# The inverse transform in quarters of the array, and two moved steps

## The chip, the cores and the metric

The kernel runs on one core of one Trainium2 chip. The metric is the device time of one execution in microseconds; lower is better. All data are float32 except two small bfloat16 tables.

## The reference

The input x has shape (8, 384, 64, 64): eight batch elements, 384 channels, 64 x 64 positions. Two residual layers follow each other.

```python
# layer 0: linear attention on group-normalised x
q, k = rope(Wq @ gn(x) + bq), rope(Wk @ gn(x) + bk);  v = Wv @ gn(x) + bv
q = elu(q * scale) + 1;  k = elu(k) + 1                 # 6 heads of 64
out = (q @ (k^T v)) / (q . sum(k) + 1e-6)
x = x + Wfc @ out + bfc

# layer 1: gated convolution with a filter in the Fourier space of 8x8 patches
t = w_in @ gn(x)
t = irfft2(rfft2(t in 8x8 patches) * fft_filter)
t = depthwise 3x3 convolution of t with w_dw
x = x + w_out @ (gelu(t[:192]) * t[192:])
```

## The kernel before

Names of engines: PE multiplies matrices, DVE (vector) and ACT (scalar) work elementwise, POOL is the GpSimd engine, SP issues most transfers. The kernel is written in a tile framework: instructions are listed in program order, and the framework places the waits and may issue a later instruction of an engine first, where an earlier one isn't ready by its own reckoning. So the order of an engine's queue is not only that of the source.

The 4096 positions of an element are split into eight bands of 512 (eight image rows). The 384 channels lie in three tiles of 128 partitions. A band of x is one tile of 128 x 3 x 512, in a ring of ten. All products go through one pool of eight PSUM banks (`ps_tile`); three of these (`acc`) are held while an element's keys are summed up.

Per element, the work has these stages:

- `norm_chain`: group statistics to a scale and a shift per channel, by tiny matmuls on PE (`ps_m`, `ps_mc`, `ps_v`, `ps_r`) with steps of DVE and one of ACT between. It is a generator; each `yield` lets other work in.
- Keys: `k_project` (`pk`, with `px` transposing x), rotation and elu on DVE and ACT, `kx_accumulate` (`acc`).
- `queries`: for each band the projection (`pq`), a normaliser (`pn`, `prb`), and the output (`pf`) added to x.
- Layer 1, per band j: `normalised` (ACT), `expand_filter` with the projection `pi`, the forward transform `pd` in 64x64 quarters and the filter on DVE (`tf`); `back_transform` (`pb`, ACT copies into `ring`); then `first_taps` on ACT and `taps` on DVE (`dw`), `gate_taps` (`gated`), and `contract` (`pw`, added to x and stored).

The layer-1 bands of element b are interleaved with the key stage of element b + 1, whose matmuls fill PE. Taps of band j - 1 wait for band j, for the row below, which POOL copies between the two `ring` tiles. The last band of an element is gated and contracted (`gate`, `output`) inside the next element's `queries`. The last element has no next one: its layer-1 bands run alone, with two bands' third channel tile convolved on PE (`ptap`).

`idft` before is 128 x 128 with the 64 x 64 inverse transform twice on its diagonal. The 128 partitions of `tf` are the 64 coefficients of two rows of patches, so one matmul inverts 128 channels of both, and its output has the patches in 64-column pieces.

At the start, the eight bands of x are loaded on SP, band 0 in three pieces; then `wk`. The constant `bk_bc` (a bias spread to all partitions) goes through ACT's queue. `sum_weight(wk)` (`pg_wk`) adds up the weight's rows by group, for the bias; it stands within the first parameter chain, after its fourth step.

Of the kernel before, what the change touches and what calls it, by code (L numbers as in the profile page):

```python
# [14 lines left out]
P = 128  # L15
C = 384
CT = 3
H = W = 64
N = H * W
NBAND = 8  # L20
BT = N // NBAND
# [18 lines left out]
def shape_constants():  # L40

    f32 = np.float32
    c = {}
    grp = np.arange(C) // GROUP
    member = (grp[:, None] == np.arange(C // GROUP)[None, :]).astype(f32)

    by_tile = member.reshape(CT, P, -1).transpose(1, 0, 2).reshape(P, -1)
    c["groups"] = np.concatenate([by_tile / f32(GROUP), by_tile, np.eye(P, dtype=f32)], 1)
    c["of_group"] = np.ascontiguousarray(member.T)

    dim = C // 2
    inv = (1.0 / np.power(f32(10000.0), np.arange(0, dim, 2, dtype=f32) / f32(dim))).astype(f32)
    ang = (np.arange(H, dtype=f32)[:, None] * inv[None, :]).astype(f32)
    cos, sin = np.cos(ang).astype(f32), np.sin(ang).astype(f32)
    sgn = np.where(np.arange(QC) < QC // 2, -1.0, 1.0).astype(f32)
    ssin = sin * sgn[None, :]


    tok = np.arange(N).reshape(NBAND, 4, P)
    tk = np.stack([np.stack([t[tok // W], t[tok % W]], 3) for t in (cos, ssin)], 1)  # L60
    c["tk"] = np.ascontiguousarray(tk.transpose(3, 0, 1, 2, 4, 5))


    half, within = QPERM // (C // 2), QPERM % (C // 2)
    freq = within // 2
    partner_sign = np.where(within < QC, -1.0, 1.0).astype(f32)
    n = np.arange(N)
    pos = np.where(half[:, None] == 0, n[None, :] // W, n[None, :] % W)
    cq = cos[pos, freq[:, None]].reshape(CT, P, NBAND, BT)
    sq = (sin[pos, freq[:, None]] * partner_sign[:, None]).reshape(CT, P, NBAND, BT)  # L70

    c["tq"] = np.ascontiguousarray(np.stack([cq[0], sq[0], cq[1], sq[1]], 2))

    c["cq2"] = np.ascontiguousarray(cq[2, :, 0, :W])
    c["sq2"] = np.ascontiguousarray(sq[2, :, 0, :W])

    e = np.zeros((4, 32, C + 2), f32)
    for part in range(3):  # L80
        e[:, part * NH + QPERM // HD, np.arange(C)] = 1.0
        e[:, part * NH : (part + 1) * NH, C:] = -(part > np.arange(2)).astype(f32)
    c["expand"] = e.reshape(P, C + 2)


    coefs = []
    for v in range(5):
        for u in range(8):
            if v in (0, 4):
                if u in (0, 4):  # L90
                    coefs.append((u, v, 0, 1.0))
                elif u < 4:
                    coefs += [(u, v, 0, 2.0), (u, v, 1, 2.0)]
            else:
                coefs += [(u, v, 0, 2.0), (u, v, 1, 2.0)]
    assert len(coefs) == 64
    pp, qq = np.arange(64) // 8, np.arange(64) % 8
    fwd = np.zeros((64, 64))
    bwd = np.zeros((64, 64))
    fsel = np.zeros((40, 64))  # L100
    for k, (u, v, part, a) in enumerate(coefs):
        th = 2 * np.pi * ((u * pp + v * qq) % 8) / 8
        fwd[:, k] = np.sin(th) if part else np.cos(th)
        bwd[k] = fwd[:, k] * a / 64
        if v in (0, 4):
            fsel[u * 5 + v, k] += 0.5
            fsel[(-u % 8) * 5 + v, k] += 0.5
        else:
            fsel[u * 5 + v, k] = 1.0
    c["dft"] = np.concatenate([fwd, fwd]).astype(f32)  # L110
    c["idft"] = np.kron(np.eye(2), bwd).astype(f32)
    c["fsel"] = np.concatenate([fsel, fsel], 1).astype(f32)
    return c

# [2 lines left out]
def conv_blocks_kernel(ctx: ExitStack, tc: tile.TileContext, a: dict, out: bass.AP, nb: int):  # L117
# [10 lines left out]
    def ps_tile(name):  # L128
        return psum.tile([P, 512], F32, tag="ps", name=name)
# [9 lines left out]
    def load_x(b, j):  # L139
        if b >= nb:  # L140
            return
        t = xp.tile([P, CT, BT], F32, tag="x", name=f"x_{b}_{j}")
        if b == j == 0:
            for m in range(CT):
                nc.sync.dma_start(t[:, m], x_in[b][:, m, j * BT : (j + 1) * BT])
        else:
            nc.sync.dma_start(t, x_in[b][:, :, j * BT : (j + 1) * BT])
        xt[b, j] = t

    stats, moments = {}, {}  # L150
# [56 lines left out]

    group_w = {}

    for j in range(NBAND):  # L210
        load_x(0, j)

    k_runs = ((0, 0, C),)
# [2 lines left out]
    def load_weight(b, name, runs):  # L216
        if b >= nb:
            return None
        if name in ("wk", "wq"):
            t = small.tile([P, CT, C], F32, tag=name, name=f"{name}_{b}", bufs=1)  # L220
        else:
            t = w_tile([P, CT, C], f"{name}_{b}")
        for c0, at, n in runs:
            nc.sync.dma_start(t[:, :, at : at + n], w_in_dram[name][:, :, c0 : c0 + n])
        return t


    def const_tile(shape, name, src, queue=nc.scalar):
        t = const.tile(shape, F32, tag=name, name=name)
        queue.dma_start(t, src)  # L230
        return t
# [7 lines left out]
    )  # L239
    ident = groups[:, 2 * CT * NG :]  # L240
    of_group = const_tile([NG, C], "of_group", a["of_group"])
    bk_bc = const_tile([P, C], "bk_bc", a["bk"].partition_broadcast(P))
    first_wk = load_weight(0, "wk", k_runs)
    scale = HD ** -0.5
    halves = (slice(0, 64), slice(64, P))
    w_out = const.tile([P, 2, C], F32, tag="w_out", name="w_out")
# [399 lines left out]

    def back_transform(b, j, tf):
        t = ring[j % 2]
        for m in range(CT):
            p_ = ps_tile(f"pb_{b}_{j}_{m}")  # L650
            patches = p_.rearrange("p (s u i n) -> p s i u n", s=2, u=2, i=2)
            for k in range(4):
                nc.tensor.matmul(  # L653
                    patches[:, k // 2, k % 2],
                    tf[:, k, m * P : (m + 1) * P],
                    idft.rearrange("p (u n) -> p u n", u=2),
                    start=True,
                    stop=True,
                )
            nc.scalar.copy(  # L660
                t[:, m, 1:9, 1 : W + 1].rearrange("p r (b c) -> p r b c", c=8),
                p_.rearrange("p (b r c) -> p r b c", b=8, r=8),
            )
        if j == 0:
            nc.gpsimd.memset(t[:, :, 0, :], 0.0)
        else:
            before = ring[(j - 1) % 2]
            nc.gpsimd.tensor_copy(t[:, :, 0, :], before[:, :, 8, :])
            nc.gpsimd.tensor_copy(before[:, :, 9, :], t[:, :, 1, :])  # L669
        if j == NBAND - 1:  # L670
            nc.gpsimd.memset(t[:, :, 9, :], 0.0)
# [54 lines left out]
        taps(b, j)  # L726
        gate_taps(b, j)

    def contract(b, j):
        g = gated  # L730
        x_ = xt.pop((b, j))
        adding = b == nb - 1 and j < NBAND - 1
        y = w_tile([P, CT, BT], f"y_{b}_{j}") if adding else None
        to = x_out[b][:, :, j * BT : (j + 1) * BT]
        for m in range(CT):
            p_ = ps_tile(f"pw_{b}_{j}_{m}")
            for s in range(2):
                nc.tensor.matmul(  # L738
                    p_, w_out[:, s, m * P : (m + 1) * P], g[:, s, :], start=(s == 0), stop=(s == 1)
                )  # L740
            if adding:
                nc.scalar.copy(y[:, m, :], p_)
            else:
                nc.vector.tensor_add(x_[:, m, :], p_, x_[:, m, :])  # L744
                if b == nb - 1:
                    nc.sync.dma_start(to[:, m], x_[:, m, :])
        if adding:

            nc.gpsimd.dma_start(out=x_, in_=y, accum_op=ALU.add)
        if adding or b < nb - 1:  # L750
            nc.sync.dma_start(to, x_)

    def layer0_chain(b, prepared):

        if b >= nb:
            return
        wk = load_weight(b, "wk", k_runs) if b else first_wk
        params = []
        for i, _ in enumerate(norm_chain(b, 0, params)):
            if b == 0 and i == 3:  # L760
                sum_weight(wk, "wk")
            yield
        scale_weight(wk, params)
        yield
        prepared += params, wk, k_bias(b, params)
# [44 lines left out]
    def queries(b, keys, gate, output):  # L810
# [12 lines left out]
        for j in range(NBAND):  # L823
# [16 lines left out]
            if j >= 1:  # L840
# [4 lines left out]
                run(output_)  # L845
                if j < NBAND - 2:
                    next(chain, None)
            if j == 2:
                output()
            if j in (4, 5):  # L850
                load_x(b + 1, j - 4)
# [30 lines left out]
    bfc = const_tile([P, CT], "bfc", a["bfc"], nc.sync)  # L882
    w_in = weight("w_in", nc.sync)
    dft = const_tile([P, 64], "dft", a["dft"], nc.sync)
    idft = const_tile([P, P], "idft", a["idft"], nc.sync)
    w_dw = const_tile([P, CT, 9], "w_dw", a["w_dw"], nc.sync)
    nc.sync.dma_start(w_out[:, 0, :], a["w_out"][0:P, :])
    nc.sync.dma_start(w_out[64:P, 1, :], a["w_out"][P : P + 64, :])
# [29 lines left out]
    for b in range(nb):  # L918
# [1 line left out]
        keys = Keys(b + 1, prepared)  # L920
        params = []
        chain, more = norm_chain(b, 1, params), chain_of(keys.project(0), keys.project(1))
        for steps in (2, 1, 1, 3):
            next(chain)
            for _ in range(steps):
                next(more, None)
        run(chain)
        ahead = normalised(b, 0, params, (8, 8), "f")
        run(more)
        if b == nb - 1:  # L930
            break
        first_sums = chain_of(keys.accumulate(0), keys.accumulate(1))
        for j in range(NBAND + 1):
# [104 lines left out]
```

## Time and profile before

| | |
|---|---|
| median of 3 runs | 3505.67 us (3504.19 to 3510.26) |
| the profiled execution | 3504.77 us, span 3503.0 us |
| granted PE clock, mean | 0.994 |
| PE busy | 3438.7 us, 98% of the span |
| DVE busy | 2894.7 us, 83% |
| ACT busy | 1805.7 us, 52% |
| HBM read / written | 232.44 MB / 50.33 MB |

The profile is of one execution. A row of its group list names the source line, the engine, the operation, output and inputs by tile name, the shape and the count, then busy time and the mean duration of one instruction, then the idle time ahead of them and what ended it. PE's records overlap: a record's duration holds its pipeline, so the step from start to start tells the pace. A float32 matmul has two records. PEld is the loading of weights. The chain that ended last is followed back from the end of the span.

### The profile page before, as it was taken

How to read it: one execution, taken by the hardware profiler on the slowest of the kernel's cores; microseconds unless marked ns; L12 is line 12 of the kernel's file. 1: busy time of each engine (PE TensorE's matmuls, PEld its weight loads, DVE VectorE, ACT ScalarE, POOL GpSimd, SP SyncE). 2: the span in 40 equal slices, each digit the busy share in tenths (PEclk: the TensorE clock that was granted, in tenths of full speed). 3: DMA queues.
4: the chain of work that ended last, by engine and by line, in shares of the span. 5: the costliest groups of instructions: out<-in, count | busy, mean ns of one | idle time of the engine just before them, and what ended most of it. 6: DMA issues, size and time to landing. Idle time of an engine off the chain costs nothing.

```text
span 3503.0 us, 38501 instructions
## 1 busy us (share of the span) xinstructions
PE 3438.7 (98%) x14384; PEld 1872.3 (53%) x14384; DVE 2894.7 (83%) x4499; ACT 1805.7 (52%) x3242; POOL 128.3 (4%) x305
## 2 busy tenths in 40 slices
PE   8999999999999999999999999999999999999998
PEld 5545565455554556545565455644555446554454
DVE  7586998868988699886998869987799877998688
ACT  4445563456544565445553555635655354534553
POOL 0000000000000000000000000000000000000011
PEclk9999999999999999999999999999999999999999
DMA  6321233212332122321223212232123211222013
GB/s 214 110 70 52 73 101 113 76 52 73 109 109 84 49 81 90 117 79 46 99 73 129 67 45 100 94 108 67 46 99 116 97 56 34 75 80 88 15 45 90
DMA packets 124641, 290.76 MB, mean 83 GB/s; under 512 B 26101, under 2 KB 36518, under 8 KB 116262
## 3 DMA queue, kind: packets, MB, share of 16 engines
q1 hardware_dynamic: 123110, 282.39, 23.9%
q0 software_dynamic: 1008, 5.51, 0.8%
q8 instruction: 113, 1.85, 0.2%
q14 instruction: 74, 0.61, 0.1%
q10 hardware_dynamic: 336, 0.41, 0.0%
HBM read 232.44 MB, written 50.33 MB: 81 GB/s over the span
## 4 chain that ended last, share of the span: by engine, by line
PE 79%; DVE 12%; issue 4%; ACT 3%; POOL 1%; DMA 1%; ACTq 0%; POOLq 0%
PE pq L525 15%; PE pf L604 15%; PE acc L445 12%; PE pk L430 11%; PE pi L622 8%; DVE dw L714 7%; PE pw L738 7%; PE pb L653 3%; PE pd L636 2%; PE px L396 1%; PE pn L563 1%; DVE kc L437 1%; ACT ring L660 1%; POOL ring L669 1%; DVE x L744 1%
## 5 line engine op out<-in xcount | busy, mean ns | idle before, releaser
L714 DVE SCALAR_TENSOR_TENSOR dw<-ring,w_dw,dw 128x512 f32<-128x512 f32 x1520 | 1054.8, 747 | 118.5 <-ACT dw L700 96.1
L430 PE MATMUL pk<-wk,x 128*128 128x384 f32 x1536 | 542.8, 493 | 0.1
L525 PE MATMUL pq<-x,wq 128*128 128x512 f32 x1152 | 520.2, 599 | 0.7
L604 PE MATMUL pf<-qc,mt 128*128 128x512 f32 x1152 | 513.7, 599 | 0.0
L622 PE MATMUL pi<-w_in,hf 128*128 128x384 f32 x1536 | 509.8, 489 | 2.2 <-ACT hf L330 1.4
L445 PE MATMUL acc<-xk,kc 128*128 128x385 f32 x1488 | 502.4, 490 | 9.0 <-DVE kc L337 9.0
L445 PEld LDWEIGHTS acc<-xk,kc 128*128 128x128 f32 x1488 | 279.9, 190 | 227.1 <-issue 46.5
L622 PEld LDWEIGHTS pi<-w_in,hf 128*128 128x128 f32 x1536 | 290.6, 191 | 200.6 <-issue 5.5
L430 PEld LDWEIGHTS pk<-wk,x 128*128 128x128 f32 x1536 | 279.2, 192 | 177.2 <-issue 21.5
L525 PEld LDWEIGHTS pq<-x,wq 128*128 128x128 f32 x1152 | 212.8, 190 | 252.3 <-issue 234.6
L604 PEld LDWEIGHTS pf<-qc,mt 128*128 128x128 f32 x1152 | 213.4, 190 | 249.6 <-issue 232.5
L738 PE MATMUL pw<-gated,w_out 128*128 128x512 f32 x768 | 343.0, 596 | 0.6 <-DVE gated L722 0.6
L397 ACT COPY xk<-px 128x384 f32<-128x384 f32 x248 | 116.4, 478 | 343.1 <-PE px L396 342.2
L629 ACT COPY ht<-pi 128x384 f32<-128x384 f32 x256 | 121.5, 475 | 234.0 <-PE pi L622 233.4
L608 DVE SCALAR_TENSOR_TENSOR x<-pf,bfc,x 128x512 f32<-128x512 f32 x192 | 141.1, 743 | 107.5 <-PE pf L604 106.8
L738 PEld LDWEIGHTS pw<-gated,w_out 128*128 128x128 f32 x768 | 141.5, 191 | 159.0 <-issue 141.9
L653 PE MATMUL pb<-idft,tf 128*128 128x128 f32 x1536 | 188.9, 278 | 11.6 <-DVE tf L644 11.6
L653 PEld LDWEIGHTS pb<-idft,tf 128*128 128x128 f32 x1536 | 181.7, 193 | 31.2 <-DVE tf L644 20.7
L433 DVE TENSOR_TENSOR kc<-pk,kbias 128x384 f32<-128x384 f32 x256 | 141.1, 551 | 68.3 <-PE pk L430 67.0
L660 ACT COPY ring<-pb 128x512 f32<-128x512 f32 x192 | 109.7, 580 | 158.1 <-PE pb L653 157.4
L335 ACT ACTIVATE qs<-qc 128x1536 f32<-128x1536 f32 x64 | 95.0, 1484 | 170.5 <-DVE qc L554 160.5
L335 ACT ACTIVATE ks<-kc 128x1536 f32<-128x1536 f32 x64 | 95.0, 1485 | 136.1 <-DVE kc L437 124.4
(153 smaller groups left out, 4032.2 us busy)
## 6 DMA issues: line engine op xcount, KB each, us to landing
tq<-in_tq SPq DMA_DIRECT2D x64, 1024.0 KB, 4.8
tk<-in_tk SPq DMA_DIRECT2D x64, 768.0 KB, 4.3
x<-in_x SPq DMA_DIRECT2D x63, 768.0 KB, 4.6
out_dram<-x SPq DMA_DIRECT2D x63, 768.0 KB, 3.3
xs<-in_x SPq DMA_DIRECT2D x56, 768.0 KB, 5.1
x<-y POOLq DMA_DIRECT2D x7, 768.0 KB, 5.7
wk<-in_wk SPq DMA_DIRECT2D x8, 576.0 KB, 4.0
wv<-in_wv SPq DMA_DIRECT2D x8, 576.0 KB, 6.1
```

Of the source, the lines that this page charges most:

```text
L335: nc.scalar.activation(e, x_, AF.Relu, scale=-1.0)
L430: nc.tensor.matmul(pk[:, :C], tokens(t), wks[:, t, :], start=(t == 0), stop=(t == CT - 1))
L433: nc.vector.tensor_add(kc[:, i, :], pk[:, :C], bias)
L445: nc.tensor.matmul(acc[m][:, : C + 1], kf[:, i, m * P : (m + 1) * P], xk[:, i, :], start=(j == 0 and i == 0), stop=(j == NBAND - 1 and i = ...
L525: nc.tensor.matmul(p_, wqs[:, t, m * P : (m + 1) * P], xt[b, j][:, t, :], start=(t == 0), stop=(t == CT - 1),)
L604: nc.tensor.matmul(p_, mt[:, t, m * P : (m + 1) * P], q[:, t, :], start=(t == 0), stop=(t == CT - 1))
L608: nc.vector.scalar_tensor_tensor(xm, p_, bfc[:, m : m + 1], xm, ALU.add, ALU.add)
L622: nc.tensor.matmul(p_[:, :C], h[:, t, i * P : (i + 1) * P], w_in[:, t, :], start=(t == 0), stop=(t == CT - 1),)
L653: nc.tensor.matmul(patches[:, k // 2, k % 2], tf[:, k, m * P : (m + 1) * P], idft.rearrange("p (u n) -> p u n", u=2), start=True, stop=True,)
L660: nc.scalar.copy(t[:, m, 1:9, 1 : W + 1].rearrange("p r (b c) -> p r b c", c=8), p_.rearrange("p (b r c) -> p r b c", b=8, r=8),)
L714: nc.vector.scalar_tensor_tensor(acc[:, m], src, wd, acc[:, m], ALU.mult, ALU.add)
L738: nc.tensor.matmul(p_, w_out[:, s, m * P : (m + 1) * P], g[:, s, :], start=(s == 0), stop=(s == 1))
```

## The change

In `back_transform`, the inverse transform runs in four quarters of the PE array. `idft` is the 64 x 64 matrix in both halves of the partitions. Each of the two row halves of `tf` writes its own bank, and each 64 channels of a tile write one half of the partitions. Channel tiles 0 and 1 share one pair of banks, 256 columns each; tile 2 has another pair. The copies into `ring` are two per channel tile, of 256 columns.

`contract` is split into a generator, `contraction`, that yields after each channel tile's matmuls and then adds and stores. For the last element, the contraction of the element before (its band 7) leaves `queries` and is interleaved with the last element's parameter chain.

At the start, band 0 is one transfer, `wk` is loaded ahead of band 7, `bk_bc` goes behind it on SP's queue, and `sum_weight(wk)` precedes the first parameter chain.

```diff
-    c["idft"] = np.kron(np.eye(2), bwd).astype(f32)
+    c["idft"] = np.concatenate([bwd, bwd]).astype(f32)
...
-        if b == j == 0:
-            for m in range(CT):
-                nc.sync.dma_start(t[:, m], x_in[b][:, m, j * BT : (j + 1) * BT])
-        else:
-            nc.sync.dma_start(t, x_in[b][:, :, j * BT : (j + 1) * BT])
+        nc.sync.dma_start(t, x_in[b][:, :, j * BT : (j + 1) * BT])
...
-    for j in range(NBAND):
+    for j in range(NBAND - 1):
         load_x(0, j)
...
-    bk_bc = const_tile([P, C], "bk_bc", a["bk"].partition_broadcast(P))
     first_wk = load_weight(0, "wk", k_runs)
+    load_x(0, NBAND - 1)
+    bk_bc = const_tile([P, C], "bk_bc", a["bk"].partition_broadcast(P), nc.sync)
...
     def back_transform(b, j, tf):
         t = ring[j % 2]
-        for m in range(CT):
-            p_ = ps_tile(f"pb_{b}_{j}_{m}")
-            patches = p_.rearrange("p (s u i n) -> p s i u n", s=2, u=2, i=2)
-            for k in range(4):
-                nc.tensor.matmul(
-                    patches[:, k // 2, k % 2],
-                    tf[:, k, m * P : (m + 1) * P],
-                    idft.rearrange("p (u n) -> p u n", u=2),
-                    start=True,
-                    stop=True,
-                )
-            nc.scalar.copy(
-                t[:, m, 1:9, 1 : W + 1].rearrange("p r (b c) -> p r b c", c=8),
-                p_.rearrange("p (b r c) -> p r b c", b=8, r=8),
-            )
+        for m0, m1 in ((0, 2), (2, 3)):
+            ps = [ps_tile(f"pb_{b}_{j}_{m0}_{u}").rearrange("p (m s i n) -> p m s i n", m=2, s=2, i=2) for u in range(2)]
+            for m in range(m0, m1):
+                for k in range(4):
+                    for c in range(2):
+                        for u, half in enumerate(halves):
+                            nc.tensor.matmul(
+                                ps[u][halves[c], m - m0, k // 2, k % 2],
+                                tf[half, k, m * P + 64 * c : m * P + 64 * c + 64],
+                                idft[half, :],
+                                start=True,
+                                stop=True,
+                            )
+                rows = t[:, m, 1:9, 1 : W + 1].rearrange("p r (s u i c) -> p u r s i c", s=2, u=2, i=2)
+                for u in range(2):
+                    nc.scalar.copy(rows[:, u], ps[u][:, m - m0].rearrange("p s i (r c) -> p r s i c", r=8))
...
-    def contract(b, j):
+    def contraction(b, j):
...
+        ps = []
         for m in range(CT):
             p_ = ps_tile(f"pw_{b}_{j}_{m}")
             for s in range(2):
                 nc.tensor.matmul(
                     p_, w_out[:, s, m * P : (m + 1) * P], g[:, s, :], start=(s == 0), stop=(s == 1)
                 )
+            ps.append(p_)
+            yield
+        y = w_tile([P, CT, BT], f"y_{b}_{j}") if adding else None
+        to = x_out[b][:, :, j * BT : (j + 1) * BT]
+        for m, p_ in enumerate(ps):
             if adding:
...
+    def contract(b, j):
+        run(contraction(b, j))
...
-        for i, _ in enumerate(norm_chain(b, 0, params)):
-            if b == 0 and i == 3:
-                sum_weight(wk, "wk")
-            yield
+        if b == 0:
+            sum_weight(wk, "wk")
+        yield from norm_chain(b, 0, params)
...
-            if j == 2:
+            if j == 2 and b < nb - 1:
                 output()
...
-    idft = const_tile([P, P], "idft", a["idft"], nc.sync)
+    idft = const_tile([P, 64], "idft", a["idft"], nc.sync)
...
-        for steps in (2, 1, 1, 3):
+        last = b == nb - 1
+        if last:
+            more = contraction(b - 1, NBAND - 1) if b else iter(())
+        for steps in (2, 0, 1, 1) if last else (2, 1, 1, 3):
             next(chain)
             for _ in range(steps):
                 next(more, None)
```

## The prediction

> **What bounds the kernel now.** I read the page first (busy shares, the chain that ended last, the costly groups), then windows by stage, then the timeline around one inverse transform, then the chain at the two ends of the span.
>
> The page:
>
> ```profile
> PE 3438.7 (98%) x14384; PEld 1872.3 (53%) x14384; DVE 2894.7 (83%) x4499; ACT 1805.7 (52%) x3242; POOL 128.3 (4%) x305
> PE 79%; DVE 12%; issue 4%; ACT 3%; POOL 1%; DMA 1%; ACTq 0%; POOLq 0%
> L653 PE MATMUL pb<-idft,tf 128*128 128x128 f32 x1536 | 188.9, 278 | 11.6 <-DVE tf L644 11.6
> L660 ACT COPY ring<-pb 128x512 f32<-128x512 f32 x192 | 109.7, 580 | 158.1 <-PE pb L653 157.4
> ```
>
> PE is busy 98% and carries 79% of the chain. The inverse transform (pb) is 189 us of it. Two records stand for each f32 matmul, so 24 per band (3 channel tiles x 4 token groups x 2) and 64 bands. ACT idles before the first ring copy of all 64 bands.
>
> The windows below are bands of layer 1 in one batch element: one early band, then four later ones that share the time with the next element's keys (columns: window, length, PE, PEld, DVE, ACT):
>
> ```profile
> 1208.10:1226.00 17.90, 17.90 (x84) 11.12 (x84) 12.14 (x19) 10.04 (x22) 0.68 (x1) 1.00 0.16 52
> 1247.50:1275.90 28.40, 27.15 (x114) 15.85 (x113) 28.10 (x45) 11.39 (x21) 1.40 (x3) 1.00 0.40 139
> 1275.90:1315.40 39.50, 37.69 (x144) 21.30 (x142) 37.50 (x52) 28.18 (x52) 0.82 (x3) 0.96 0.27 88
> 1315.40:1349.60 34.20, 34.20 (x138) 20.54 (x138) 32.66 (x49) 20.84 (x36) 1.12 (x3) 1.00 0.26 89
> 1349.60:1383.60 34.00, 34.00 (x138) 20.36 (x137) 30.43 (x44) 19.83 (x36) 1.38 (x4) 1.00 0.28 93
> ```
>
> PE is full in some bands, but DVE is as full in the second and third row and has only 1.5 to 3.6 us left in the last two. So time saved on PE is not all time of the kernel. I count five of eight bands of an element as PE-paced (the first two and the last three), three as DVE-paced, and all eight of the last element, where the chain is 47% DVE taps and PE is busy 163 of 187 us.
>
> The timeline of one early band:
>
> ```profile
> 1197.88 2.10 PE L445 MATMUL acc<-xk,kc 128*128 128x385 f32 x6
> 1199.91 0.21 PEld L636 LDWEIGHTS pd<-ht,dft 64*64 64x64 f32 x8 [0.55 <-ACT hf L330]
> 1199.91 1.52 PE L636 MATMUL pd<-ht,dft 64*64 64x384 f32 x16
> 1201.36 4.15 PE L445 MATMUL acc<-xk,kc 128*128 128x385 f32 x12
> 1205.35 2.84 PE L653 MATMUL pb<-idft,tf 128*128 128x128 f32 x24
> 1206.44 0.59 ACT L660 COPY ring<-pb 128x512 f32<-128x512 f32 x1 [5.19 <-PE pb L653]
> ```
>
> The forward transform (pd) already runs in quarters: 16 records of 64x64 take 1.52 us, four rounds of 0.32 us, each round one pass of 384 columns in all four quarters at once. Its first eight loads fit in 0.21 us although one lasts 0.13.
>
> **The change, part by part.**
>
> *Matmuls.* The 2 records of a tile and group (128 rows, 128 columns) become 8 (four quarters x two), 64 columns each: 96 records a band, 24 rounds of four. Before, 24 records take 2.68 us by the chain (0.112 each). For a round, the nearest row is pv, 64 columns moving and 64 columns of weights on two half arrays:
>
> ```profile
> 183.98 0.57 PE L492 MATMUL pv<-xks,wv 128*64 128x64 f32 x12
> ```
>
> Six rounds in 0.57, less the 0.22 that the last record lasts, is five steps of about 0.06; I take 0.058. Four quarters a round should cost no more, as pd's rounds show. So 24 x 0.058 = 1.4 us a band. [...]
>
> *Switching between whole array and quarters.* New before and after pb where pd and pb are apart. From the timeline: the last acc record starts at 1197.88 + 2.10 - 0.49 = 1199.49, streams 0.32, and pd starts 0.10 after that, with 0.05 more for its first weights; pd's last round ends streaming at 1201.27, acc starts at 1201.36, and its twelve records take 0.11 over 11 x 0.323 + 0.487. So 0.15 in, 0.20 out, 0.35 a band. [...]
>
> *Two tiles in one bank.* Channel tiles 0 and 1 share two banks, one for each row half; ACT copies tile 0 out before tile 1 is written. No row of before shows a bank being read while PE writes it. [...] A copy of 128x256 lies between rows of 128x128 (0.29) and 128x384 (0.475): 0.38. Reckoned from where the previous work ends streaming: tile 0 runs 0.15 to 0.61, its last record ends near 0.80, copies run 0.82 to 1.59, tile 2 (own banks) can run 0.61 to 1.07, tile 1 runs 1.63 to 2.09, next work streams at 2.29. That is 2.68 - 2.29 = 0.39 us gained a band. If a whole-array matmul fills the wait, the price is a second switch: 1.4 + 0.70 = 2.1, a gain of 0.6. The order of PE isn't fixed by the source: in before a contraction matmul already stands between two pb groups at 3382 us. With no wait at all, 0.95. With tile 2 after tile 1, 2.75: nothing. I take 0.5 and keep -0.1 to 0.95.
>
> *Copies on ACT.* Six of 0.38 for three of 0.58: +0.54 us a band. ACT is 52% busy, so on PE-paced bands the rest of its work covers it. On DVE-paced bands the chain runs tf, pb, ring copies, the POOL halo copy, taps. There the first copy starts 0.1 to 0.2 sooner (0.82 for 0.93), and the last ends 0.4 later: cost up to 0.4, perhaps half on average.
>
> *The last contraction of the seventh element* leaves the last element's queries (12 records, 5.3 us, PE gapless there) for its final parameter chain, where PE is nearly idle:
>
> ```profile
> 3316.20 0.34 PE ps_m L271 x6
> 3320.29 1.45 PE ps_r L279 x6
> 3322.21 0.82 ACT hf L330
> 3323.08 10.29 PE pi L622 x24
> ```
>
> From 3313.07 to 3323.08 PE does 3 us of work, and then pi takes 10.29 where 7.74 is usual; loads 0.64 apart then show a clock that had dropped. Gain: 5.3. Against it: the first two tiles take 3.6 us from 3313, so ps_m (ready 3.1 after) waits 0.5; the third tile's 1.8 us can delay ps_mc or ps_v by about 0.6; three DVE adds of 0.69 stand among the chain's 0.15 us steps and may cost 0.3 each; together 2. A clock kept up may give back 0 to 2.5. Net gain 3 to 6; I take 4.5. The output DMA of that band moves along on SP; nothing waits for it.
>
> *The start.* Bands of x land until 21.5 us, and the parameters wait for the last. Weight wk (576 KB) ahead of band 7 delays it; 6.3 MB in about 19 us is 330 KB/us, so +1.75, less 0.55 for bk_bc's copies, which go behind it on SP. Gain: wk's sums are off the chain.
>
> ```profile
> 27.42 3.59 PE L343 MATMUL pg_wk<-wk,groups 128*32 128x384 f32 x6
> 30.94 0.82 PE L279 MATMUL ps_r<-rsg,of_group 32*128 32x1 f32 x6
> ```
>
> The scale was ready at 28.9, and ps_r waited 2.0 for pg_wk. Now pg_wk falls into PE's idle time while statistics run. Band 0 in one transfer lands whole at 8, as its third part did; DVE catches up by 10, when band 1 comes. SP saves two issues and gains one. Net -0.8, between -2 and +1.5. The smaller constant and its DMA cost nothing; SP has finished them long before the first pb at 346.
>
> *Sum.* 35 PE-paced bands x 0.5 = -17.5; 29 DVE-paced, of which some 20 lie on the chain through the ring, x 0.2 = +4; end -4.5; start -0.8: -19. The profiled execution took 3504.8 (span 3503.0 and 1.8 around it), 0.9 under the median 3505.7, so about 3487. A measurement of this kernel can tell some 0.2%, 7 us.
>
> **The rivals.**
>
> *No bank wait (chance 0.18).* If tile 1's writes pass the copies, or long work fills the wait at no second switch, 0.95 x 35 = 33, and DVE-paced bands give 0.3 x 29 = 9; with the ends 47: 3459. For: pd shows quarters running freely. [...]
>
> *The handover only pays itself back (0.15).* Tile 2 kept behind tile 1: no PE gain, +4 from ACT, -5 from the ends: 3505, no change.
>
> *ACT is late at the handover: slower (0.27).* [...] In the band at 1366 ACT had only 0.19 us idle before the first copy, after 2.2 us of normalising and a 0.46 us copy of transposes, and between ring copies stood a 0.72 us statistics pass with its 0.19 readout. One such pass between the two copies adds 0.9: the gain of 0.4 turns into a loss of 0.5, +18 on 35 bands, and 0.6 on 20 chained ones, +12; less 5: 3530. It decides from a wait of about 0.95 us a band beyond tile 2. Against: the 157 us of ACT idle before first copies, 2.5 a band.
>
> **How the numbers follow.** The forecast gets 0.40 (3472 to 3500), and with its spread beside the rivals: faster by over 7 us 0.57, within 0.13, slower 0.30. The range takes in the no-wait case and most of the late-ACT case: 3450 to 3525. The faster cases alone span 3450 to 3498.
>
> **What would show it.** pb should have 6144 records and rounds near 0.058 us; a PE gap or a foreign matmul ahead of tile 1; 384 ring copies near 0.38. [...] pi at the start of the last element should drop from 10.3 towards 8, and ps_r should follow the scale at once in the first 35 us. PE idle in pb above 1.5 us a band would prove the slower rival.

## The result, and the profile after

The changed kernel takes 3502.91 us (median of 20 runs, 3500.72 to 3505.61), the kernel before beside it 3505.49 us (20 runs, 3503.68 to 3510.26): ratio 0.9989 [0.9983, 0.9995], a gain of 2.6 us. That is under the 0.2% that the prediction called no change, though the interval leaves out 1. I had forecast a gain of 19. The time lies in the range; the size is wrong.

The page of the changed kernel (rows as in the prediction):

```profile
span 3501.5 us, 47938 instructions
PE 3419.7 (98%) x18992; PEld 1818.5 (52%) x18992; DVE 2885.2 (82%) x4499; ACT 1833.9 (52%) x3448; POOL 101.8 (3%) x305
L654 PE MATMUL pb<-idft,tf 64*64 64x64 f32 x6144 | 151.1, 227 | 26.0 <-DVE tf L641 8.7
L663 ACT COPY ring<-pb 128x256 f32<-128x256 f32 x384 | 122.6, 395 | 174.2 <-PE pb L654 172.4
```

PE has lost 19 us of busy time, 38 of them at pb, but the span only 1.5. The idle time before pb went from 11.6 to 26.0. The chain of this page covers only the end of the span (PE 2%), so it can't be set against the one before.

The same early band as in the prediction, timeline of PE and ACT:

```profile
1201.82 4.15 PE L442 MATMUL acc<-xk,kc 128*128 128x385 f32 x12
1205.90 0.92 PE L654 MATMUL pb<-idft,tf 64*64 64x64 f32 x44
1206.65 0.67 ACT L663 COPY ring<-pb 128x256 f32<-128x256 f32 x2 [4.93 <-PE pb L654]
1207.09 1.31 PE L654 MATMUL pb<-idft,tf 64*64 64x64 f32 x52 [0.27 <-ACT ring L663]
1208.09 1.23 ACT L663 COPY ring<-pb 128x256 f32<-128x256 f32 x4 [0.78 <-PE pb L654]
1208.33 0.91 PE L619 MATMUL pi<-w_in,hf 128*128 128x384 f32 x2
```

Of the 96 records 44 go at once; then PE stands until a ring copy lets it go on. From the first record to the next work it is 1208.33 - 1205.90 = 2.43 us, for 2.68 before. ACT's two copies of a tile, 0.39 us each, overlap: 0.67 together.

The bands of one element, as in the prediction (after the four engines come POOL, the granted clock of PE, the DMA share and GB/s):

```profile
1208.30:1226.20 17.90, 17.63 (x158) 10.32 (x155) 12.25 (x19) 10.50 (x25) 0.26 (x1) 1.00 0.21 61
1247.50:1276.20 28.70, 27.01 (x185) 14.90 (x184) 28.53 (x45) 10.51 (x23) 1.45 (x3) 1.00 0.39 134
1276.20:1315.00 38.80, 36.50 (x216) 20.80 (x214) 38.29 (x53) 29.30 (x56) 1.43 (x3) 0.96 0.29 94
1315.00:1349.30 34.30, 33.73 (x210) 19.58 (x211) 30.73 (x46) 20.10 (x38) 0.75 (x3) 1.00 0.27 86
1349.30:1383.50 34.20, 33.99 (x210) 19.78 (x209) 30.07 (x44) 20.10 (x38) 0.74 (x3) 1.00 0.28 93
```

Against before, the bands' lengths hardly moved (the third lost 0.7 us, the others at most 0.3 either way); in the second and third row DVE is busy for all but 0.2 and 0.5 us.

The last parameter chain:

```profile
3307.49 3.60 PE L737 MATMUL pw<-gated,w_out 128*128 128x512 f32 x8
3311.02 0.35 PE L268 MATMUL ps_m<-mv,groups 128*32 128x1 f32 x6
3312.68 1.99 PE L737 MATMUL pw<-gated,w_out 128*128 128x512 f32 x4
3314.59 0.35 PE L268 MATMUL ps_v<-d,groups 128*32 128x1 f32 x6
3316.64 1.07 PE L276 MATMUL ps_r<-rsg,of_group 32*128 32x1 f32 x6 [1.70 <-DVE rsg L305]
3319.01 10.41 PE L619 MATMUL pi<-w_in,hf 128*128 128x384 f32 x24 [1.30 <-ACT hf L327]
```

pi starts at 3319.01, 4.1 sooner than before, and still takes 10.4 us.

The start:

```profile
19.68 2.10 PE L340 MATMUL pg_wk<-wk,groups 128*32 128x384 f32 x6
28.14 1.40 PE L276 MATMUL ps_r<-rsg,of_group 32*128 32x1 f32 x6 [1.47 <-DVE rsg L305]
30.96 3.57 PE L427 MATMUL pk<-wk,x 128*128 128x384 f32 x5
```

ps_r is freed of pg_wk, as foreseen, and the first keys (pk) start at 30.96 for 32.64 before. Yet the first pi of layer 1 comes at 332.6 us, for 331.4 before; experiments 7 and 8 come back to this.

### The profile page after: what moved, and what is told of

Same layout as the page of the kernel before. It is cut to its first block, busy times and chain, and to the rows that moved or that the text cites. A ratio compares the mean times of both kernels' runs of the same rounds, so it can differ in the third digit from the quotient of the medians.

```text
span 3501.5 us, 47938 instructions
## 1 busy us (share of the span) xinstructions
PE 3419.7 (98%) x18992; PEld 1818.5 (52%) x18992; DVE 2885.2 (82%) x4499; ACT 1833.9 (52%) x3448; POOL 101.8 (3%) x305
## 5 line engine op out<-in xcount | busy, mean ns | idle before, releaser
L427 PE MATMUL pk<-wk,x 128*128 128x384 f32 x1536 | 551.2, 498 | 5.5 <-DVE kc L430 2.5
L737 PE MATMUL pw<-gated,w_out 128*128 128x512 f32 x768 | 350.7, 602 | 2.4 <-DVE tf L641 1.8
L663 ACT COPY ring<-pb 128x256 f32<-128x256 f32 x384 | 122.6, 395 | 174.2 <-PE pb L654 172.4
L654 PE MATMUL pb<-idft,tf 64*64 64x64 f32 x6144 | 151.1, 227 | 26.0 <-DVE tf L641 8.7
L654 PEld LDWEIGHTS pb<-idft,tf 64*64 64x64 f32 x6144 | 127.6, 135 | 77.1 <-DVE tf L641 23.8
L173 ACT ACTIVATE differences<-x,shift 128x512 f32<-128x512 f32 x168 | 119.9, 714 | 77.0 <-DVE x L605 77.0
```

What stands on the lines that cost most here:

```text
L427: nc.tensor.matmul(pk[:, :C], tokens(t), wks[:, t, :], start=(t == 0), stop=(t == CT - 1))
L654: nc.tensor.matmul(ps[u][halves[c], m - m0, k // 2, k % 2], tf[half, k, m * P + 64 * c : m * P + 64 * c + 64], idft[half, :], start=True, ...
L663: nc.scalar.copy(rows[:, u], ps[u][:, m - m0].rearrange("p s i (r c) -> p r s i c", r=8))
L737: nc.tensor.matmul(p_, w_out[:, s, m * P : (m + 1) * P], g[:, s, :], start=(s == 0), stop=(s == 1))
```

## The experiments

Times are medians; ratios are to the kernel before on the same chip. I follow an element by the starts of its first pi from band to band, and PE by its time from start to start of its records, summed by tile name (a stall counts for the tile ahead of it).

**1 to 4: the parts alone, and the handover.** Theory 1: the two tiles in one bank make PE wait for ScalarE's copies, and that eats the gain. Rival: small matmuls, switching or the smaller copies cost it.

*copies_last*: the changed kernel; both tiles' matmuls precede the copies of their pair, so no matmul waits for a copy.

```diff
+            for m in range(m0, m1):
                 rows = t[:, m, 1:9, 1 : W + 1].rearrange(...)
                 for u in range(2):
                     nc.scalar.copy(rows[:, u], ps[u][:, m - m0]...)
```

> The changed kernel with the two ring copies of a channel tile issued after the matmuls of both tiles of the pair, so that no matmul waits for a copy of its own bank. Theory 1 (the handover in the shared bank eats what the quarters save on PE): the group of 96 pb records has no gap and goes from its first start to the next record in about 1.5 us (2.43 in the changed kernel), and the kernel gains 0.9 us on some 35 PE-paced bands: 25 to 40 us under the changed kernel. Theory 2 (PE's saved time isn't the kernel's, since DVE and ACT pace the layer-1 bands): the group shortens alike, but the kernel stays within 8 us of the changed one.

*quarters_only*: the kernel before with only the new `back_transform` and `idft`.

```diff
-    idft = const_tile([P, P], "idft", a["idft"], nc.sync)
+    idft = const_tile([P, 64], "idft", a["idft"], nc.sync)
...
+        for m0, m1 in ((0, 2), (2, 3)):
...
```

> The kernel before with the changed inverse transform alone. Theory 1: within 3 us of the kernel before, since the handover pays back what the rounds save (2.43 us plus 0.25 of switching for 2.68). If the ends carry the changed kernel's 2.6 us, this one is 0 to 2 us slower than before; if the quarters carry it, it is 2 to 4 us faster.

*start_only*: the kernel before with only the new start.

```diff
-    for j in range(NBAND):
+    for j in range(NBAND - 1):
         load_x(0, j)
...
+    load_x(0, NBAND - 1)
...
+        if b == 0:
+            sum_weight(wk, "wk")
+        yield from norm_chain(b, 0, params)
```

> The kernel before with the changed start alone (loads, bk_bc's queue, the weight's sums ahead of the chain). Theory 3 (the sums had kept PE's clock up through the chain): the first k projection starts 1.7 us sooner but its first matmuls step at 0.64 us, and at the first layer-1 band the kernel is 1.2 us later: 1 to 1.5 us slower in all. The forecast's reckoning: 0.8 us faster.

*end_only*: the kernel before with only the moved contraction.

```diff
-            if j == 2:
+            if j == 2 and b < nb - 1:
                 output()
...
+        if last:
+            more = contraction(b - 1, NBAND - 1) if b else iter(())
+        for steps in (2, 0, 1, 1) if last else (2, 1, 1, 3):
```

> The kernel before with the contraction moved into the last parameter chain alone. The forecast's reckoning: 3 to 6 us faster. From the changed kernel's trace, where the last element's first projection began 2.8 us sooner against the start of the last queries and took as long as before: about 3.5 us faster, with pi's first 24 records still at 10.3 us.

| | us | ratio, 95% |
|---|---|---|
| copies_last | 3482.87 | 0.9936 [0.9923, 0.9948] |
| quarters_only | 3508.06 | 1.0009 [1.0001, 1.0018] |
| start_only | 3507.01 | 1.0 [0.9992, 1.0008] |
| end_only | 3501.42 | 0.999 [0.9982, 0.9999] |

One line moved is worth 20 us against the changed kernel, where theory 1 expected 25 to 40. The timeline of copies_last:

```profile
348.81 1.63 PE L654 MATMUL pb<-idft,tf 64*64 64x64 f32 x96
350.02 1.78 ACT L664 COPY ring<-pb 128x256 f32<-128x256 f32 x6 [5.40 <-PE pb L654]
350.37 1.88 PE L619 MATMUL pi<-w_in,hf 128*128 128x384 f32 x5
```

All 96 records run in one piece, 1.56 us to the next work. So rounds and switching cost what I had said, and theory 1 holds: the same quarters, in the same shared banks, lose 0.87 us in such a band to the handover, and bands 0 and 1 of an element, where nothing else differs, are 0.86 us shorter. But the gain is less than pb's: PE's time at pb fell from 181.6 us (before) to 121.9, while the time at pd rose from 140.8 to 168.9. Experiments 9 to 12 follow that.

The quarters as written, alone, gain 3.7 us over six elements (from +3.4 us against before at the first pi to -0.3 at the seventh element's; the first of them loses 1.0), and give it back after that: +2.4 at the last element's first pi, +7.2 at the end of the span. The trace is of an execution of 3512.01 us, 4 above the median, so a part of the 7.2 is its own. The +3.4 arises at the start, whose code is that of before: its first pk comes at 33.46 for 32.64, and pg_wk takes 4.03 for 3.59. Experiments 7 and 8 show why kernels with one start code differ so much there.

**5, 6: is it the bank or the copies' size?** *six_banks*: the changed kernel, each tile with its own two banks.

```diff
-        for m0, m1 in ((0, 2), (2, 3)):
+        for m0, m1 in ((0, 1), (1, 2), (2, 3)):
```

> The changed kernel with a pair of banks for each channel tile, so that no tile shares a bank, and each tile's copies still directly behind its own matmuls. Theory 1 (the shared bank makes the handover): tile 1 no longer waits; with three banks held for the keys only five of eight are free, so tile 2 may wait for the release of tile 0's, which by then is 0.1 to 0.4 us away: pb 1.6 to 2.0 us a band for 2.43, and the kernel 8 to 18 us faster than before. Rival (it is the placing of the copies on ACT, not the bank): within 3 us of the changed kernel.

*split_copies*: the kernel before, its ring copy of 512 columns cut into two of 256, as a control for ACT's six smaller copies.

```diff
+            for h in range(2):
-                t[:, m, 1:9, 1 : W + 1].rearrange("p r (b c) -> p r b c", c=8),
-                p_.rearrange("p (b r c) -> p r b c", b=8, r=8),
+                t[:, m, 1:9, 1 + 32 * h : 33 + 32 * h].rearrange("p r (b c) -> p r b c", c=8),
+                p_[:, 256 * h : 256 * h + 256].rearrange("p (b r c) -> p r b c", b=4, r=8),
```

> The kernel before, whole-array transform, with each ring copy of 512 columns split into two of 256. It prices the doubled copies alone: some 192 x (2 x 0.39 - 0.58) = 38 us more of ACT. The forecast put +4 us on the kernel for it (0.2 us on 20 bands that hang on the ring). If ACT had room everywhere: 0. If the copies' latency were on every band: 64 x 0.2 = 13.

six_banks took 3496.32 us, 0.9968 [0.9956, 0.9981], 9 us under before, as theory 1 expected. In the early band pb took 1207.23 - 1205.42 = 1.81 us, so not sharing the bank gives 0.62 of the 0.87. `acc` holds three of the eight banks, and six are more than the five left, which may be the rest; that was not tested.

split_copies took 3489.2 us, 0.995 [0.9936, 0.9964]: 16 us *faster*, where no gain was expected. Bands 0, 1 and 6 of its fifth element are as long as before to 0.01 us, so the six copies cost nothing there, and something else had moved. ACT in the kernel before, in a band of the third element:

```profile
1284.54 1.28 ACT L336 ACT_TABLE_LOAD   x1
1285.84 1.48 ACT L336 ACTIVATE ks<-ks 128x1536 f32<-128x1536 f32 x1
1287.34 1.28 ACT L721 ACT_TABLE_LOAD   x1
1288.63 0.63 ACT L721 ACTIVATE gated<-dw 64x512 f32<-64x512 f32 x1
1289.29 0.48 ACT L629 COPY ht<-pi 128x384 f32<-128x384 f32 x1
```

And in split_copies:

```profile
1274.22 0.63 ACT L722 ACTIVATE gated<-dw 64x512 f32<-64x512 f32 x1 [1.09 <-DVE dw L715]
1277.76 1.28 ACT L336 ACT_TABLE_LOAD   x1
1279.05 1.48 ACT L336 ACTIVATE ks<-ks 128x1536 f32<-128x1536 f32 x1
1280.44 0.46 ACT L629 COPY ht<-pi 128x384 f32<-128x384 f32 x1
```

In the kernel before, a Gelu half stands behind the exp, with a table load of its own, ahead of the last copy to ht; the last six records of pd start at 1290.62. In split_copies the half comes before the exp. The framework chose another order; its own reckoning of the times is the likely reason, which no run here shows.

**7, 8: the ends again.** *last_oldstart*: copies_last with the start of before (its edit is that of start_only, undone).

> Copies behind both tiles' matmuls, the moved contraction, and the start as before the change. Theory 3 (the new start costs 0.6 us of its own and nothing is gained by it): 0 to 2 us faster than the kernel with copies last, 3481 to 3483. The forecast's reckoning of the start (0.8 us gained) would make it 0.8 us slower.

*keep_warm*: copies_last, with idle matmuls in the first and the last chain, to hold PE's clock. They stand for no part of the computation.

```diff
+        def keep_warm(src, moving, name):
+            if warm:
+                p_ = ps_tile(name)
+                for _ in range(2):
+                    nc.tensor.matmul(p_[: src.shape[1], :320], src, moving, start=True, stop=True)
...
+        keep_warm(d, groups[:, :320], f"warm_d{n}")
...
+        keep_warm(rsg, of_group[:, :320], f"warm_r{n}")
```

> The kernel with copies last, with four more matmuls of 320 columns, whose results nobody reads, in the first parameter chain and in the last element's: two behind ps_v, two behind ps_r. Theory 3 (PE's clock falls in the thin chain, and the first projection behind it runs slow until it is back: 2.7 us at the start, 1.8 to 2.4 in the last element): pk's and pi's first matmuls step at 0.32 us for 0.64 and the kernel gains 2 to 4 us on the one with copies last (3482.9): 3479 to 3481. If the clock does not come back from this little work, or the extra matmuls delay the chain: same or up to 2 us slower.

last_oldstart took 3483.38 us, 0.9933 [0.992, 0.9945]: no difference. keep_warm took 3486.67 us, 0.9944 [0.9931, 0.9956], 3.8 more than copies_last. Its timeline at the start:

```profile
27.65 2.29 PE L290 MATMUL warm_d<-groups,d 128*3 128x320 f32 x4
29.87 1.44 PE L276 MATMUL ps_r<-rsg,of_group 32*128 32x1 f32 x6
31.24 2.29 PE L290 MATMUL warm_r<-of_group,rsg 32*1 32x320 f32 x4
```

The windows from 20 to 40 us (granted clock third from the end) of before, of quarters_only, which has the same start, and of the changed kernel:

```profile
20.00:40.00 20.00, 15.98 (x66) 9.47 (x65) 11.23 (x33) 4.18 (x9) 0.00 (x0) 0.83 0.60 193
20.00:40.00 20.00, 16.10 (x54) 8.59 (x53) 8.13 (x29) 4.17 (x9) 0.00 (x0) 0.66 0.60 189
20.00:40.00 20.00, 15.34 (x51) 8.73 (x50) 8.82 (x29) 2.85 (x6) 0.00 (x0) 0.74 0.60 185
```

In keep_warm the clock is 0.66 too, as in copies_last. It falls to half at 24.9 us, before the added matmuls start (27.65), and they only delay ps_r. So keep_warm failed to hold the clock, and doesn't say what a held clock would bring. What the traces do show is where the new start's gain went: the keys begin 1.7 us sooner in the changed kernel, at a lower clock than in before. The new start alone doesn't make the clock lower, since three kernels with before's start have 0.66. The first pi of layer 1 follows the clock (us, one execution each; columns by start code):

| clock, 20 to 40 us | start of before | new start |
|---|---|---|
| 0.91 | 330.3 split_copies, 330.6 end_only | |
| 0.83 | 331.4 before | 331.4 fewer_taps |
| 0.74 | | 332.0 start_only, 332.6 changed kernel, 333.0 six_banks |
| 0.66 | 334.5 last_oldstart, 334.6 taps_before, 334.8 quarters_only | 333.4 copies_last, 333.7 taps_after, 333.8 taps_last |

At 0.66 the new start is 1.0 us ahead, at 0.83 level. Down the column of before's start the time grows by 4 us as the clock falls, down the other by 2.

**9 to 11: ACT's order made equal.** Theory A: what pd lost in copies_last, and won in split_copies, comes from Gelu halves and table loads standing between the copies to ht. The edit puts the taps of tiles 0 and 2 in turn, so that both Gelu halves become ready together. The program's table loads are 117 in before, 131 in the changed kernel and in copies_last, and 103 with the edit in each of them.

```diff
-        for m in range(CT - on_array(b, j)):
-            for k in range(1, 9):
+        order = [(m, k) for m in range(CT - on_array(b, j)) for k in range(1, 9)]
+        if not on_array(b, j):
+            order = [(m, k) for k in range(1, 9) for m in (0, 2)] + [(1, k) for k in range(1, 9)]
+        for m, k in order:
```

*taps_before*: this edit in the kernel before.

> Kernel before, with one edit: in the bands whose three channel tiles all take their taps on VectorE, the taps of tiles 0 and 2 are issued in turn, then tile 1's, so that both Gelu halves on ScalarE become ready together. In ScalarE's program the table loads fall from 117 to 103 (1.283 us each). Theory A (the stretch at pd comes from the Gelu halves and their table loads standing between the copies to ht): pd's share of PE's time falls from 141 us to some 127, as in split_copies, and the time from 3505 to 3487-3495. Theory B (what split_copies gained came from the smaller copies themselves): no gain, 3502-3508.

*taps_after*: in the changed kernel.

> Changed kernel with the same edit of the order of taps; table loads fall from 131 to 103. Beside taps_before it gives the change's effect with the order on ScalarE equal. Theory A: 3480-3492, pw's share back from 343 us to about 333. The change itself by its parts (end -4, start +1, inverse transform about 0) would then be -2 to -6 against taps_before. Theory B: 3500-3505.

*taps_last*: in copies_last.

> copies_last with the same edit of the order of taps; table loads fall from 131 to 103. Theory A: pd's share falls from 169 us to 130-140 and pw's from 340 to about 333, so the time from 3483 to 3440-3460. Rival: the waits at pd come from ScalarE's six copies of 128x256 standing before the next band's copies to ht, whatever the Gelu does: pd stays above 160, 3475-3484.

| | us | ratio, 95% |
|---|---|---|
| taps_before | 3486.52 | 0.9949 [0.9937, 0.9961] |
| taps_after | 3506.02 | 1.0 [0.9992, 1.0008] |
| taps_last | 3475.78 | 0.9915 [0.9901, 0.9928] |

Theory A holds in the main for the kernel before (19 us; in the element below all of it in band 4), falls for the changed one, and gives copies_last 7 of the 23 or more expected. In band 4, PE's time falls from 5.03 us (before) to 2.43 (taps_before) at pd, and by another 1.1 at acc and pk. At acc and pk the clock plays a part, which theory A had left out. In before:

```profile
2146.70:2150.11 3.41, 1.59 (x11) 0.49 (x4) 3.38 (x5) 3.36 (x5) 0.00 (x0) 1.00 0.35 136
2150.11:2153.52 3.41, 3.41 (x10) 1.06 (x9) 2.20 (x6) 0.30 (x1) 0.00 (x0) 0.50 0.00 0
```

After the stands at pd, in a window of 3.41 us with 1.59 of PE, PE's clock is halved (0.50) for 3.41 us. In before this happens in band 4 of the second to the sixth element; in taps_before and split_copies the clock stays full through these elements.

The lengths of the bands of the fifth element show what the edit moves in each kernel (us from pi to pi, from the traces; after band 7 the queries follow):

| band | before | taps_before | after | taps_after | copies_last | taps_last | fewer_taps |
|---|---|---|---|---|---|---|---|
| 0 | 17.99 | 17.99 | 17.83 | 17.83 | 16.97 | 16.97 | 16.97 |
| 1 | 17.89 | 17.89 | 17.83 | 17.60 | 16.97 | 16.97 | 16.97 |
| 2 | 21.58 | 21.58 | 21.38 | 22.04 | 21.07 | 21.73 | 21.72 |
| 3 | 28.37 | 28.50 | 28.70 | 30.22 | 30.31 | 28.39 | 29.36 |
| 4 | 39.55 | 35.87 | 38.84 | 36.47 | 36.30 | 36.88 | 36.09 |
| 5 | 34.15 | 34.14 | 34.23 | 35.51 | 35.20 | 35.35 | 33.22 |
| 6 | 34.04 | 34.44 | 34.23 | 33.98 | 33.66 | 33.11 | 33.47 |

The cheap handover takes 1.0 us off bands 0 and 1 and 1.3 off band 6 (taps_last against taps_before), and gives 2.1 back in bands 3 to 5. Bands 3 to 5 of taps_last:

```profile
2088.70:2117.10 28.40, 25.50 (x185) 14.40 (x184) 28.20 (x45) 11.15 (x27) 1.34 (x3) 1.00 0.31 108
2117.10:2154.00 36.90, 34.87 (x217) 19.70 (x215) 36.63 (x51) 28.96 (x56) 1.64 (x3) 1.00 0.32 111
2154.00:2189.30 35.30, 33.67 (x209) 19.46 (x209) 32.86 (x49) 20.16 (x38) 0.74 (x3) 1.00 0.29 96
```

In the first row PE idles 2.9 us and DVE 0.2, in the second 2.0 and 0.3. In the third DVE is gapless for the first 19 us, in which PE stands twice for DVE's kc; later DVE idles 2.4:

```profile
2166.55 2.20 PE L427 MATMUL pk<-wk,x 128*128 128x384 f32 x6 [0.84 <-DVE kc L430]
2173.44 0.69 PE L654 MATMUL pb<-idft,tf 64*64 64x64 f32 x30 [0.79 <-DVE kc L430]
```

In taps_after, band 4 gains 2.4 us on the changed kernel, but bands 2, 3 and 5 lose 3.5. In band 3 PE stands 2.27 us for the gated product, and then its clock is halved:

```profile
2116.20 1.52 PE L633 MATMUL pd<-ht,dft 64*64 64x384 f32 x16
2119.99 7.08 PE L739 MATMUL pw<-gated,w_out 128*128 128x512 f32 x12 [2.27 <-DVE gated L724]
```

In taps_last nearly the same wait at the same place costs nothing more, 5.42 for 7.08 us:

```profile
2100.31 5.42 PE L740 MATMUL pw<-gated,w_out 128*128 128x512 f32 x12 [2.24 <-DVE gated L725]
```

The windows show a difference. In the traces of before and of the changed kernel the granted clock changes 17 and 15 times, and each change lies a whole multiple of 3.4133 us after the trace's first clock record (up to 1022 and 1023 of them, to 0.01 of one). Windows on such a grid around the wait, two of taps_after and two of taps_last:

```profile
2116.63:2120.04 3.41, 1.14 (x17) 0.35 (x9) 3.41 (x7) 0.16 (x1) 0.00 (x0) 0.99 0.52 195
2120.04:2123.45 3.41, 3.41 (x4) 1.47 (x5) 2.42 (x5) 0.00 (x0) 0.00 (x0) 0.51 0.03 7
2096.15:2099.56 3.41, 1.92 (x18) 0.56 (x16) 3.41 (x6) 0.48 (x1) 0.00 (x0) 1.00 0.73 229
2099.56:2102.97 3.41, 2.66 (x6) 1.25 (x7) 3.41 (x8) 0.00 (x0) 0.00 (x0) 1.00 0.00 1
```

In taps_after the wait lies inside one window, which PE fills for a third (1.14 of 3.41), and the next window has half the clock. In taps_last it lies across the border of two, each filled for more than half (1.92 and 2.66), and the clock stays at 1.00. So a band's length in the table holds the clock's luck too: band 4 of before and of the changed kernel, and band 3 of taps_after, copies_last and fewer_taps, each hold one halved window, while taps_before and taps_last hold none in this element.

**12: DVE as the bound.** *fewer_taps*: taps_last without the centre tap of bands 2 to 4, so with less work for DVE beside bands 3 to 5. The convolution lacks a term there.

```diff
+        if b < nb - 1 and j in (2, 3, 4):
+            order = [(m, k) for m, k in order if k != 4]
```

> taps_last with the centre tap of bands 2, 3 and 4 of elements 0 to 6 left out (it runs beside the inverse transforms of bands 3 to 5), so the convolution of those bands lacks one term: 63 VectorE instructions of 0.66 us from start to start, 2.0 us less a band, 42 us in all. Table loads stay at 103. In taps_last VectorE is busy 28.2 of 28.4, 36.6 of 36.9 and 32.9 of 35.3 us of those bands in element 4, PE 25.5, 34.9 and 33.7. Theory (VectorE sets the length of these bands, so that PE's saved time there goes into waits): the bands get up to 2 us shorter each, and the time falls from 3476 to 3436-3456. Rival (ScalarE's order, or PE, sets it): 3466-3477.

It took 3458.81 us, 0.9858 [0.9842, 0.9874]: 17.0 us less than taps_last, between the theory's 20 to 40 and the rival's 10 at most. In the traces 2.4 of it lie at the start, where the clock differs, so the bands gave some 15. Band 5:

```profile
2142.20:2175.40 33.20, 33.20 (x209) 19.25 (x210) 28.32 (x42) 19.70 (x38) 0.75 (x3) 1.00 0.29 96
```

With 2 us of DVE's work left out of each of the three bands, DVE reaches this one less behind (42 of its instructions fall in the band, for 49), PE's two stands for kc are gone, PE is gapless, and the band is 2.1 us shorter. There the theory is shown. Band 4 gained 0.8, and band 3 got 1.0 longer: in it the clock fell this time (PE's time at pw 7.04 us for 5.35), as in taps_after; in the third element, where it didn't, band 3 was 28.51 for 28.39, no shorter either. So for band 3 a bound by DVE's sum of work is not shown.

## Why the prediction was right and wrong

- *Rounds and switching: right.* 0.058 us a round was taken; starts in the trace step by 0.058. The four records of a round start 7 ns apart, and a band of 96 records takes 1.56 us in copies_last.
- *The shared bank: the wait right, size wrong.* That tile 1's matmuls wait for both copies of tile 0 was the prediction's estimate, which no trace of before shows. In the changed kernel the wait view names ring copies as releasers of pb (us in total, times, longest):

```profile
PEld pb L654 <- ACT ring L663: 21.8, 48, 1.5
```

The failed step is the first term of the sum, 35 PE-paced bands at 0.5 us, and in it first the "I take 0.5". It let all of tile 2 run while PE waits. In the early band 44 records run before the wait. Tile 0 has 32 of a band's 96, so only 12 of tile 2's 32 can be among them (the trace doesn't name the tiles). The other 20 started only after the stand, 0.49 us from the last start before it to the first after it, though they need no copy. No run shows the 0.5: the uncut pb gained 0.25, and bands 0 and 1 got 0.16 and 0.06 shorter.
- *35 PE-paced bands: the count failed too.* In the fifth element the five bands so counted (0, 1, 5, 6, 7) gave 0.0 us together, for 2.5 forecast. Bands 5 and 6 got 0.1 and 0.2 longer: in band 6 PE's time at pb fell by 0.25, but rose by 0.25 at pd and by 0.1 each at pk and px. The three DVE-paced ones (2 to 4), for which a cost was forecast, gave 0.6.
- *Copies on ACT: mis-sized.* 0.54 us more a band was taken; ACT's busy time at the ring copies rose by 12.9 us, 0.20 a band, since copies in a row overlap (two of 0.39 us in 0.67).
- *The last element was mis-sized.* The prediction put its bands at small costs on the chain through the ring. From its first pi to the end of the span the changed kernel lost 2.6 us (from 4.1 ahead to 1.5); copies_last lost 0.4 (from 22.3 to 21.9).
- *The end: right.* 4.5 was taken; end_only gained 4.0 at pi. Nothing came back from the clock: pi still takes 10.4.
- *The start: mis-sized by the clock.* -0.8 was taken. start_only gave +0.6 at the first layer-1 band, and last_oldstart said -1.1 for the new start. At equal clock the traces give -1.0 (0.66, three kernels each) and 0.0 (0.83, one pair), near the term. What I had not seen is the halved clock beside the thin chain, with which the start moves by 4 us under one start code. The changed kernel's trace has the lower clock of the two, which is luck as far as these traces tell.
- *The sum,* by the first pi of each element against before: start +1.3, six elements -3.8, end -4.0 (from end_only), last element +2.6. The seventh element with its queries is what is left to -1.5, the difference of the spans: +2.4, of which 1.8 show from its first pi to its last.
- *Rivals.* The no-wait case named the prize, 0.95 a band; copies_last realised 1.0 in bands 0 and 1. I had let its DVE-paced bands gain 0.3 each; taps_last shows that they lose (1.1 in bands 2 to 4 against taps_before). The late-ACT case did not come: in the wait view above the longest wait is 1.5 us, but the mean is 0.45.

The version that beats both kernels here is taps_last, 30 us faster than the kernel before. What stays open: why bands 4 and 5 of the quarter kernels are *longer* than taps_before's rather than equal, and why the seventh element lost. DVE's bound is shown for band 5 and the halved clock for band 3. How much of the time between kernels is the clock's was not taken apart, nor what else the framework reordered.

## What to carry to other kernels

When two tiles share a PSUM bank, issue both tiles' matmuls before the first copy: here that one line was worth 20 us, and 0.87 us in an early band, where work that needs no copy had stood behind the wait. Count what a faster engine can give only in the stages where it is the bound, with the other engine's busy time written beside each band. Read the granted clock of a band before its length is put down to the code. And where a framework orders the queues, test a change with that order held equal: here an edit that only reordered vector instructions was worth more than the whole change.

## What was not expected of the hardware

- A stand of PE of 2.2 to 2.3 us was followed by half the granted clock in taps_after and fewer_taps (12 matmul records in 7.1 us), and not in taps_last (5.4 us). In before the clock fell at 859.9, 1290.0, 1720.0, 2150.1 and 2580.2 us, each time for 3.41 us, and 126 times 3.413 us lie between one and the next. A window of 3.41 us only half idle was enough. In the 14 traces, from 60 us to 20 us before the last element's first pi, 62 such windows at full clock were followed by half clock, with PE busy for at most 0.51 of each; some 13,000 were not, with PE busy for at least 0.47. In before these are 5, with 0.47, and 939, with 0.63 or more. In the last element the border is less sharp (in the changed kernel a window at 3399.0 us with 0.60 was followed by half clock).
- An ACT table load took 1.283 us in each of the 117 rows of before and the 131 of the changed kernel. Fewer loads are no gain by themselves: taps_after has 28 fewer than the changed kernel and isn't faster, and split_copies has as many as before and is 16 us faster.
- ACT copies of 128x256 last 0.39 us, but two of them take 0.67, where one of 128x512 takes 0.58: in the changed kernel splitting the copy cost 0.09 us, not the 0.20 that the durations say.
